# A two-layer graph attention kernel: layer 0's output product of the first and the last step by ordinary products, row tile by row tile, and weight blocks and their sums placed anew

## The chip, the cores and the metric

The kernel runs on one core of a Trainium2 chip. The core has TensorE (PE, with its weight loads shown apart as PEld), VectorE (DVE), ScalarE (ACT), GpSimd (POOL) and SyncE (SP), which here only issues transfers. The metric is the device time of one execution in microseconds (us). One execution was also recorded by the profiler; times inside it are counted from its first instruction.

## The reference, cut to what matters

64 graphs of 256 nodes with 512 features go through two attention layers with a residual. Layer 0 has 4 heads and layer 1 has 8, of 64 each.

```python
h = relu(layernorm(x))
q, k, v = h @ Wq, h @ Wk, h @ Wv                  # layer 0: 512 -> 256
attn = softmax(where(adj, q @ k.T / 8, -max))     # per graph and head
x = x + (attn @ v) @ Wo + bo                      # "combination": 256 -> 512
h = relu(layernorm(x))                            # layer 1 norms once more, with gamma and beta,
x = x + attention1(h, adj | eye) @ w_out.T + b_out #   and has 512 -> 1536 and 512 -> 512
```

The combination of layer 0 is the product that the change touches: for two graphs at a time, 512 rows of 256 numbers by a 256 x 512 matrix, added to the residual.

## The kernel before, in words

**Tiles and steps.** The graphs are taken two by two, in 32 steps (`s` = 0 to 31). Activations of a step stand in tiles of 128 rows; a step has 512 rows, so four row tiles `t`, two for each graph. Everything is float32 but the masks. Each large product (`project_qk`, `project_v1`, `combine`) cuts both factors into 2 x 2 blocks and computes seven block products instead of eight, with sums of blocks prepared beforehand: `weight_sum` for weights, `act_sums0` and `act_sums1` for activations (lines 406 to 414). `PRODUCT` names the two blocks of each of the seven products, and the results are added up while they are copied out of PSUM (`evacuate`, `accumulate`). Only `project_v0` is done by ordinary products, row tile by row tile.

**The order is written by hand.** Every piece of work is put in a list by `at(period, place, fn, ...)`, and the list, sorted by place, is issued in that order on each engine. A period is one step of the steady state and is 6.2 places long; in it the layer-1 work of step p and the layer-0 work of steps p+1 and p+2 alternate on TensorE. `at_dense` puts the products at one place and the copying out (`rest`) shortly after. An engine takes its instructions strictly in this order, so an instruction that waits holds up all that stand behind it. The steady state runs from about the second step to the last but one; the places of the first steps (periods -2 to 0) and of the last (30 and 31) are given one by one.

**PSUM.** Four banks, `m0` to `m3`, take the results of products and transposes in turn (`mm_tile`). A product waits until the former contents of its bank have been copied out. Products 2, 4 and 3 accumulate in the bank of 1, 7 and 5, and wait until those have been copied out.

**The first end.** The weights of layer 1 come from DRAM in four parts (`weight_loads`; q, k, v and the output matrix, parts 0 to 3) and are transposed on TensorE, four blocks for each part: `weight_block(n, c)`, line 468, four transposes into one bank, and two copies out at line 473. Then `weight_sum` makes the three derived blocks and the changed one (line 406). In the kernel before, blocks of parts 0 to 2 stand between the products of steps 0 and 1, and those of part 3 inside the first `project_qk` of layer 1. The sums of `wqkv1[..., 0]` (q), `[..., 1]` (k) and `[..., 2]` (v) and of layer 0's output matrix `wo0` are on VectorE, those of `wo1` on GpSimd.

**Around the combination.** `weigh_out` leaves the attention output in `oT0`; `key_sums`, `invert` and `normalise` divide it by the softmax sums. `invert` (line 945) copies the reciprocals out to 128 partitions in eight transfers on SyncE (line 960), and `normalise` (line 965, GpSimd) multiplies. Then `act_sums0` and `act_sums1` make the sums of `oT0`, and `combine` computes the seven products of 128x256 each. `norm1` (lines 575, 632, 633) takes the mean of a finished row tile on VectorE and the centred rectified row on ScalarE; `norm1_rest` takes the second moments (VectorE) and, for two row tiles together, the scales on GpSimd (lines 648, 649, 585 to 587). `scale_row` (line 591, ScalarE) scales, and `transpose_h` (line 660) transposes for layer 1. `second_bias` (line 637, GpSimd) adds the output bias of layer 1 to the residual.

**The last end.** The last step has no successor to overlap with. Its combination of layer 1 is the end of the program: seven products, and four stores of a quarter of the result each (`store_block`, line 837, on SyncE).

Of the kernel before, what the change touches and what calls it, by code (L numbers as in the profile page):

```python
# [315 lines left out]
def fast_path(  # L316
# [19 lines left out]
    nc = tc.nc  # L336
# [128 lines left out]
    def weight_block(wr, n, c):  # L465
# [3 lines left out]
        for i in range(2):  # L469
            blk = A_OF[i, c // HC]  # L470
            dst = wqkv1[:, blk, c % HC, n, :] if n < 3 else wo1[:, blk, c % HC, :]
            copy = nc.vector.tensor_copy if i == 0 and c % 2 == 0 else nc.scalar.copy
            copy(dst, pw[:, i * H1:(i + 1) * H1])  # L473
# [52 lines left out]
    def neighbours_rows(s):  # L526
        rows = S[s]["rows"] = sm.tile([P, NT, P], BF, name="rows", tag="u", bufs=1)
        for t in range(NT):
            nc.vector.tensor_scalar(rows[:, t, :], onesb, S[s]["any"][:, t:t + 1], None, op0=ALU.mult)
# [182 lines left out]
    def accumulate(n, bank, region, u, last):  # L712
# [11 lines left out]
        elif n == 4:  # L724
            add(r21, bank, r21, ALU.add)  # L725
# [3 lines left out]
        sums = SUM_U_LAST if last else SUM_U  # L729
        if n in sums:  # L730
            r = region[sums[n]]
            (nc.vector if last else nc.gpsimd).tensor_tensor(r, r, u, ALU.add)  # L732

    SUM_U = {7: 3, 3: 1, 4: 2}
    SUM_U_LAST = {6: 1, 7: 3, 4: 2}
# [80 lines left out]
    def combine(s, lyr, n):  # L816
# [14 lines left out]
        at_once = s == NSTEP - 1 or (s, lyr) == (0, 0)  # L831
        return lambda: accumulate(n, bank, token_rows(st["xt"], HD), st["u"], at_once)

    def store_block(s, i, j):

        rows, cols = slice(j * NIC, (j + 1) * NIC), slice(i * HD, (i + 1) * HD)
        nc.sync.dma_start(
            out[s * G + j, :, cols].rearrange("(t p) d -> p t d", p=P), S[s]["xt"][:, rows, cols]
        )
# [197 lines left out]
    for s in range(NSTEP):  # L1037
# [6 lines left out]
        for t in range(NT):  # L1044
            at(p, 0.5 + 0.4 * t if s != 1 else 1.95 + 0.15 * t, norm0, s, t)
# [6 lines left out]
        if s < 2:  # L1052
            at(p, (AT_Q0 + 0.15, 2.72)[s], neighbours_rows, s)
# [6 lines left out]
        at(p, (AT_Q0 + 0.31, 3.75)[s] if s < 2 else 5.7, mask1, s)  # L1060
# [9 lines left out]
        for t in range(NT):  # L1070
            at_dense(p, AT_V0 + 0.14 * t + (-0.0005 if s == 0 and t == 0 else 0 if s != 1 else -0.26 if t < 2 else 0.29), 0.14, project_v0, s, t)
# [5 lines left out]
        at(p, 1.75 if s else 1.8, lambda s=s: act_sums0(S[s]["oT0"]))  # L1077
        at(p, 1.76 if s else 2.48, lambda s=s: act_sums1(S[s]["oT0"]))
        edge = 0 if s == 0 else 1 if s == NSTEP - 1 else 2
        for i, n in enumerate(SETC0 if s else SETC):  # L1080
            if edge == 1:
                at_dense(p, 1.99905 + 0.00008 * i, 0.00107, combine, s, 0, n)
            else:
                at_dense(p, AT_C0 + (-0.12 if s == 0 else 0.14) + i / 14, 1 / 14, combine, s, 0, n)
        for k in range(NT):
            at(p, ((3.315, 3.32, 3.39, 3.41), (2.2, 2.25, 2.4, 2.45), (3.79, 3.8, 3.93, 3.94))[edge][k], norm1, s, k)
            at(
                p, ((3.4, 3.42, 3.43, 3.435), (2.3, 2.35, 2.5, 2.55), (4.075, 4.22, 4.23, 4.36))[edge][k],
# [100 lines left out]
```

## Time and profile before

| what | value |
|---|---|
| median of 3 runs | 3387.38 us (3384.94 to 3389.29) |
| the profiled execution: its time | 3387.59 us |
| the profiled execution: its span, first to last instruction | 3385.8 us |
| PE busy | 3354.9 us (99% of the span) |
| DVE / ACT / POOL busy | 1954.2 / 1232.3 / 2214.4 us (58% / 36% / 65%) |
| mean granted TensorE clock | 0.998 |
| layer 0's combinations and layer 1's, 128x256 products (line 825) | 2688 instructions |

A product of float32 matrices shows as two instructions in this trace, so a block product of `combine` in layer 0 (two row tiles) is 4 instructions, and the whole combination of a step 28. Busy times of PE overlap, since a matmul starts before the one ahead has drained; the distance between two starts is what a matmul costs. Lines of the waits name the engine and line that wait, "<-", and what they waited for, then the us in total, the times and the longest. Lines of the timeline give start, length, engine, line, operation, tiles, shape and number of merged instructions, and in brackets the idle time ahead of it and its releaser.

### The profile page before, as it was taken

How to read it: one execution, taken by the hardware profiler on the slowest of the kernel's cores; microseconds unless marked ns; L12 is line 12 of the kernel's file. 1: busy time of each engine (PE TensorE's matmuls, PEld its weight loads, DVE VectorE, ACT ScalarE, POOL GpSimd, SP SyncE). 2: the span in 40 equal slices, each digit the busy share in tenths (PEclk: the TensorE clock that was granted, in tenths of full speed). 3: DMA queues.
4: the chain of work that ended last, by engine and by line, in shares of the span. 5: the costliest groups of instructions: out<-in, count | busy, mean ns of one | idle time of the engine just before them, and what ended most of it. 6: DMA issues, size and time to landing. Idle time of an engine off the chain costs nothing.

```text
span 3385.8 us, 60239 instructions
## 1 busy us (share of the span) xinstructions
PE 3354.9 (99%) x22986; PEld 2695.6 (80%) x22986; DVE 1954.2 (58%) x3476; ACT 1232.3 (36%) x2225; POOL 2214.4 (65%) x2108
## 2 busy tenths in 40 slices
PE   8999999999999999999999999999999999999999
PEld 6788888888888888788888888887888878888877
DVE  6655565555565555655655555556555565555556
ACT  3333333334433333333343333443333433333421
POOL 6666766667656677566676666765667766667642
PEclk9999999999999999999999999999999999999999
DMA  4111112221111111122111211111211112111111
GB/s 129 43 59 52 33 49 57 57 58 42 46 46 58 57 55 32 47 58 59 52 34 48 58 56 58 42 46 46 58 58 54 32 48 57 59 52 35 45 38 45
DMA packets 167975, 173.97 MB, mean 51 GB/s; under 512 B 59640, under 2 KB 112896, under 8 KB 167680
## 3 DMA queue, kind: packets, MB, share of 16 engines
q1 hardware_dynamic: 167280, 169.78, 17.1%
q8 instruction: 184, 3.01, 0.5%
q14 instruction: 111, 0.91, 0.1%
q10 hardware_dynamic: 400, 0.27, 0.0%
HBM read 85.99 MB, written 33.62 MB: 35 GB/s over the span
## 4 chain that ended last, share of the span: by engine, by line
PE 95%; DVE 1%; DMA 0%; SPq 0%; POOL 0%; ACT 0%; issue 0%; POOLq 0%; ACTq 0%
PE mm L768 33%; PE mm L825 17%; PE mm L809 11%; PE sc L859 11%; PE sc L902 10%; PE mm L795 6%; PE mm L660 3%; PE mm L935 2%; PE mm L548 0%; SPq L960 0%; DVE inv L945 0%; DMA xt<-in_x_dram 0%; DMA out_dram<-xt 0%; DVE p L883 0%; DVE bs L575 0%
## 5 line engine op out<-in xcount | busy, mean ns | idle before, releaser
L893 POOL TENSOR_TENSOR pd<-p 128x512 f32<-128x512 f32 x378 | 473.2, 1273 | 535.2 <-ACT p L888 523.2
L768 PE MATMUL mm<-hT,wqkv 128*128 128x256 f32 x3584 | 801.9, 383 | 3.8 <-DVE qk L700 2.3
L768 PEld LDWEIGHTS mm<-hT,wqkv 128*128 128x128 f32 x3584 | 676.2, 191 | 113.6 <-issue 21.6
L888 ACT ACTIVATE p<-p 128x512 f32<-128x512 f32 x768 | 457.4, 631 | 459.8 <-DVE p L883 457.0
L825 PE MATMUL mm<-wo,oT 128*128 128x256 f32 x2688 | 599.4, 381 | 3.1 <-issue 1.5
L825 PEld LDWEIGHTS mm<-wo,oT 128*128 128x128 f32 x2688 | 501.3, 190 | 82.7 <-DVE xt L721 10.7
L945 DVE RECIPROCAL inv<-mm 128x128 f32<-128x128 f32 x384 | 339.7, 926 | 367.7 <-PE mm L935 346.2
L919 ACT COPY oT<-sc 128x512 f32<-128x512 f32 x188 | 110.0, 585 | 1075.9 <-PE sc L902 1069.3
L883 DVE TENSOR_TENSOR p<-sc,n 128x512 f32<-128x512 f32 x768 | 478.8, 682 | 5.0 <-PE sc L859 5.0
L768 PE MATMUL mm<-hT,wqk 128*128 128x256 f32 x1792 | 398.5, 383 | 0.7 <-ACT wqkv L473 0.6
L809 PE MATMUL mm<-wqkv,hT 128*128 128x256 f32 x1792 | 395.5, 382 | 0.0
L965 POOL TENSOR_TENSOR oT<-oT,invb 128x512 f32<-128x512 f32 x188 | 240.0, 1277 | 222.9 <-DMA invb<-inv 220.8
L768 PEld LDWEIGHTS mm<-hT,wqk 128*128 128x128 f32 x1792 | 337.6, 191 | 57.6 <-issue 10.3
L809 PEld LDWEIGHTS mm<-wqkv,hT 128*128 128x128 f32 x1792 | 338.6, 190 | 54.5 <-issue 10.7
L859 PE MATMUL sc<-qk 64*128 64x256 f32 x3040 | 380.3, 390 | 0.0
L902 PE MATMUL sc<-p,v 128*32 128x256 f32 x6144 | 370.7, 382 | 0.0
L859 PEld LDWEIGHTS sc<-qk 64*128 64x128 f32 x3040 | 278.9, 187 | 103.0 <-issue 64.7
L732 POOL TENSOR_TENSOR xt<-xt,u 128x512 f32<-128x512 f32 x183 | 230.7, 1276 | 165.3 <-DVE xt L725 150.6
L902 PEld LDWEIGHTS sc<-p,v 128*32 128x32 f32 x6144 | 180.7, 110 | 160.9 <-issue 61.7
L721 DVE TENSOR_TENSOR xt<-mm,xt 128x512 f32<-128x512 f32 x128 | 88.2, 689 | 328.1 <-PE mm L825 328.0
L591 ACT ACTIVATE h<-h,mr,r 128x512 f32<-128x512 f32 x252 | 196.9, 807 | 127.9 <-POOL mr L587 123.6
L795 PE MATMUL mm<-wv,hT 128*128 128x256 f32 x1024 | 230.4, 383 | 0.1
(131 smaller groups left out, 3672.7 us busy)
## 6 DMA issues: line engine op xcount, KB each, us to landing
invb<-inv SPq DMA_DIRECT2D x1528, 32.0 KB, 1.9
xt<-in_x_dram SPq DMA_DIRECT2D x32, 1024.0 KB, 5.7
h<-in_x_dram SPq DMA_DIRECT2D x31, 1024.0 KB, 5.4
out_dram<-xt SPq DMA_DIRECT2D x31, 1024.0 KB, 4.5
ne<-row SPq DMA_DIRECT2D x30, 256.0 KB, 4.3
ad<-in_adj_dram SPq DMA_DIRECT2D x32, 128.0 KB, 10.9
wr<-in_L_gnn_w_qkv_dram SPq DMA_DIRECT2D x3, 1024.0 KB, 12.7
h<-in_x_dram SPq DMA_DIRECT2D x4, 256.0 KB, 3.5
```

The lines of the kernel that those rows point to most:

```text
L732: (nc.vector if last else nc.gpsimd).tensor_tensor(r, r, u, ALU.add)
L768: nc.tensor.matmul(bank[:, k, :], w[:, wa, c, k, a * P:(a + 1) * P], st["hT"][:, ba, c, :], start=first and (k, c) == (0, 0), stop=(k, c) ...
L795: nc.tensor.matmul(bank, st["hT"][:, b0 + t // NIC * step, c % HC, i:i + P], wv0[:, c, :], start=(c == 0), stop=(c == NC - 1),)
L809: nc.tensor.matmul(bank[:, t, :], st["hT"][:, ba, c, t * P:(t + 1) * P], wqkv1[:, wa, c, 2, :], start=first and (t, c) == (0, 0), stop=(t, ...
L825: nc.tensor.matmul(bank[:, t, :], oT[:, ba, c, t * P:(t + 1) * P], w[:, wa, c, :], start=first and (t, c) == (0, 0), stop=(t, c) == (NIC - ...
L859: nc.tensor.matmul(sc[g][e][:, kc, :], qk[rows, 1, k0:k0 + P], qk[rows, 0, g * N:(g + 1) * N], start=True, stop=True,)
L883: nc.vector.tensor_tensor(p[e][:, g], sc[e], neg[:, :, g, :], ALU.add)
L888: nc.scalar.activation(p[e][:, g], p[e][:, g], AF.Exp, scale=SCALE)
L893: eng.tensor_tensor(pd[:, e], p[e][:, :, 0, :], p[e][:, :, 1, :], ALU.add)
L902: nc.tensor.matmul(po[r0:r0 + 32, g, :], st[f"v{lyr}"][:, g * NIC + kc, pr * P + r0:pr * P + r0 + 32], p[r0 // DH][:, g, kc, :], start=(kc ...
L945: nc.vector.reciprocal(inv[:, i * P:(i + 1) * P], sums[:, i * P:(i + 1) * P])
L965: nc.gpsimd.tensor_tensor(dst, dst, invb, ALU.mult)
```

## The change

Three things are changed.

1. In the first and the last step, layer 0's combination is done by `combine_rows(s, t)`: for one row tile t, two ordinary products (one for each half of the 256 numbers), each of them 512 columns wide over both halves of the output, and one addition to the residual. No sums of `oT0` and of the output matrix are used there; the copied-out row tile is final, and its `norm1` is placed right behind it. The other steps keep the seven products. `weight_sum` changes block 2 of `wo0`, so for the last step this block is loaded anew in period 29.
2. At the first end the work is placed anew: `neighbours_rows` of step 0 on GpSimd, earlier; the sums of `wo0` and of `wqkv1[..., 2]` on GpSimd, the former in period 0; all weight blocks of parts 1 to 3 between the combination and the transposes for layer 1, with the first of their two copies on VectorE; the sums of `wqkv1[..., 1]` behind part 1; `mask1` of step 1 later, `second_bias` of step 0 in period 0.
3. At the last end, layer 1's combination takes its products in the order 1, 5, 2, 6, 7, 3, 4 instead of 1, 5, 2, 3, 6, 7, 4; both sums with `u` are made right after product 6, the addition after product 4 is done in two halves, and the stores of the last quarters go out in halves on SyncE and ScalarE.

```diff
@@ weight_block
-            copy = nc.vector.tensor_copy if i == 0 and c % 2 == 0 else nc.scalar.copy
+            copy = nc.vector.tensor_copy if i == 0 and (n or c == 0) else nc.scalar.copy
@@ neighbours_rows
-            nc.vector.tensor_scalar(rows[:, t, :], onesb, S[s]["any"][:, t:t + 1], None, op0=ALU.mult)
+            eng = nc.gpsimd if s == 0 else nc.vector
+            eng.tensor_scalar(rows[:, t, :], onesb, S[s]["any"][:, t:t + 1], None, op0=ALU.mult)
@@ accumulate
-            add(r21, bank, r21, ALU.add)
+            for t in range(NIC) if last else (slice(0, NIC),):
+                add(r21[:, t], bank[:, t], r21[:, t], ALU.add)
...
-    SUM_U_LAST = {6: 1, 7: 3, 4: 2}
+    SUM_U_LAST = {6: (1, 2), 7: (3,)}
@@ combine
-        at_once = s == NSTEP - 1 or (s, lyr) == (0, 0)
+        at_once = s == NSTEP - 1
@@ store_block
-        nc.sync.dma_start(
-            out[s * G + j, :, cols].rearrange("(t p) d -> p t d", p=P), S[s]["xt"][:, rows, cols]
-        )
+        dst, src = out[s * G + j, :, cols].rearrange("(t p) d -> p t d", p=P), S[s]["xt"][:, rows, cols]
+        if (i, j) != (1, 0):
+            (nc.scalar if (i, j) == (0, 1) else nc.sync).dma_start(dst, src)
+        else:
+            for t, queue in enumerate((nc.sync, nc.scalar)):
+                queue.dma_start(dst[:, t], src[:, t])
+
+    def combine_rows(s, t):
+
+        st = S[s]
+        g, r = t // NIC, t % NIC * P
+        bank = mm_tile([P, 2, HD])
+        for j, (b0, _, step) in enumerate(O_OF):
+            for c in range(HP0):
+                nc.tensor.matmul(
+                    bank, st["oT0"][:, b0 + g * step, c, r:r + P], wo0[:, j:4:2, c, :],
+                    start=(j, c) == (0, 0), stop=(j, c) == (1, HP0 - 1),
+                )
+        xt = st["xt"][:, t, :].rearrange("p (i o) -> p i o", i=2)
+        return lambda: nc.vector.tensor_tensor(xt, bank, xt, ALU.add)
@@ places
-            at(p, 0.5 + 0.4 * t if s != 1 else 1.95 + 0.15 * t, norm0, s, t)
+            at(p, 0.5 + 0.4 * t if s != 1 else 1.95 + 0.1395 * t, norm0, s, t)
-            at(p, (AT_Q0 + 0.15, 2.72)[s], neighbours_rows, s)
+            at(p, (2.9, 2.72)[s], neighbours_rows, s)
-        at(p, (AT_Q0 + 0.31, 3.75)[s] if s < 2 else 5.7, mask1, s)
+        at(p, (AT_Q0 + 0.31, 4.43)[s] if s < 2 else 5.7, mask1, s)
-            at_dense(p, AT_V0 + 0.14 * t + (-0.0005 if s == 0 and t == 0 else 0 if s != 1 else -0.26 if t < 2 else 0.29), 0.14, project_v0, s, t)
+            at_dense(p, AT_V0 + 0.14 * t + (-0.0005 if s == 0 and t == 0 else 0) if s != 1 else (4.31, 5.02, 5.16, 5.31)[t], 0.14, project_v0, s, t)
-        at(p, 1.75 if s else 1.8, lambda s=s: act_sums0(S[s]["oT0"]))
-        at(p, 1.76 if s else 2.48, lambda s=s: act_sums1(S[s]["oT0"]))
+        if 0 < s < NSTEP - 1:
+            at(p, 1.75, lambda s=s: act_sums0(S[s]["oT0"]))
+            at(p, 1.76, lambda s=s: act_sums1(S[s]["oT0"]))
-        for i, n in enumerate(SETC0 if s else SETC):
-            if edge == 1:
-                at_dense(p, 1.99905 + 0.00008 * i, 0.00107, combine, s, 0, n)
+        for i, n in enumerate(SETC0 if 0 < s < NSTEP - 1 else NORM1):
+            if edge == 0:
+                at_dense(p, 2.76 + 0.14 * i, 0.14, combine_rows, s, n)
+            elif edge == 1:
+                at_dense(p, 1.99905 + 0.00014 * i, 0.00113, combine_rows, s, n)
...
-            at_set(p, LAST_QK + 4.1, (1, 5, 2, 3, 6, 7, 4), combine, s, 1)
+            at_set(p, LAST_QK + 4.1, SETC, combine, s, 1)
-                at(p, LAST_QK + 4.1 + (3, 6, 6, 7)[n] / 7, store_block, s, i, j)
+                at(p, LAST_QK + 4.1 + (3, 6, 5, 7)[n] / 7, store_block, s, i, j)
+    at(NSTEP - 3, 4.5, lambda: nc.sync.dma_start(
+        wo0[:, 2], wo[:HP0 * P, HD:].rearrange("(c p) o -> p c o", p=P)
+    ))
-        at(-2, AT_V0, weight_sum, nc.vector, wo0, i)
+        at(0, 0.9, weight_sum, nc.gpsimd, wo0, i)
-        place = 3.3 - 3.93 + (1 + i) / 7 - 0.0005 if i < 4 else 0.2 + 0.07 * i if i < 8 else 1.62 + 0.1 * (i - 8) if i < 12 else 6.2 + 1 / 7 * (i - 12)
+        place = 3.3 - 3.93 + (1 + i) / 7 - 0.0005 if i < 4 else 1.3705 + 0.0001 * i if i < 8 else 1.525 + 0.03 * (i - 8)
-        at(-1, 3.1 + 0.01 * i, weight_sum, nc.vector, wqkv1[:, :, :, 1, :], i)
-        at(0, 0.2 + i / 7, weight_sum, nc.vector, wqkv1[:, :, :, 2, :], i)
+        at(-1, 1.379 + 0.0001 * i, weight_sum, nc.vector, wqkv1[:, :, :, 1, :], i)
+        at(-1, 1.8, weight_sum, nc.gpsimd, wqkv1[:, :, :, 2, :], i)
```

The places of `norm1`, `norm1_rest`, `scale_row` and `second_bias` in the two edge steps change with it: in the first step `norm1` stands behind each `combine_rows`, and `scale_row` between the weight blocks of parts 1 and 2; in the last step `norm1` stands behind each `combine_rows` too, and `norm1_rest` of the first row tile among them.

## The prediction

> **What bounds the kernel now.** The page's first part says TensorE: 99% of the span. A change away from the steady state can gain only what TensorE loses at the two ends, so I read its waits next, in the first 126 us and in the last 190 (us in total, times, longest).
>
> ```profile
> PE mm L468 <- ACT v L799: 2.6, 1, 2.6
> PE mm L660 <- ACT h L591: 2.5, 5, 0.8
> PE mm L768 <- DVE qk L700: 2.3, 1, 2.3
> PE mm L535 <- DVE rows L529: 1.8, 1, 1.8
> PE mm L825 <- issue: 1.5, 1, 1.5
> PE mm L468 <- ACT wo L473: 1.0, 1, 1.0
> ...
> PE mm L768 <- DVE qk L704: 1.3, 1, 1.3
> PE mm L825 <- DVE xt L721: 0.7, 1, 0.7
> PE mm L825 <- POOL oT L412: 0.4, 1, 0.4
> PE mm L660 <- ACT h L591: 0.4, 1, 0.4
> ```
>
> The first list, which is of 12 to 126 us, sums to 14.0 us with five smaller ones that are left out; the second, of 3200 us on, to 2.8. Third, the timeline, for where they lie and what follows; last, the stretches with the granted clock (length, the engines' busy us, clock, DMA share, GB/s).
>
> ```profile
> 19.85 0.71 PE L535 MATMUL mm<-identb,rows 128*128 128x128 bf16 x4 [1.79 <-DVE rows L529]
> ...
> 109.09 6.41 PE L768 MATMUL mm<-hT,wqkv 128*128 128x256 f32 x16 [2.33 <-DVE qk L700]
> ...
> 96.05 5.81 DVE L406 TENSOR_TENSOR wqkv<-wqkv 128x512 f32<-128x512 f32 x4
> ...
> 3377.28 2.00 PE L825 MATMUL mm<-wo,oT 128*128 128x256 f32 x8 [0.67 <-DVE xt L721]
> ...
> 3380.04 0.69 DVE L732 TENSOR_TENSOR xt<-xt,u 128x512 f32<-128x512 f32 x1
> ```
>
> ```profile
> 87.30:90.70 3.40, 3.31 (x14) 2.76 (x16) 1.75 (x6) 2.19 (x9) 2.57 (x8) 0.50 0.00 0
> ...
> 107.70:114.60 6.90, 5.51 (x13) 4.44 (x14) 4.10 (x6) 1.84 (x5) 6.90 (x6) 0.51 0.06 14
> ```
>
> After two of the waits TensorE runs at half clock for 3.4 and 6.8 us. At 109 us sixteen instructions take 6.41 us where 56 take 12.28 elsewhere (0.22 each, so 3.5): 2.8 us more. Around 87 to 91 us it is some 1.6. With these the first end loses about 19 us behind 12 us. The wait at 109 us is VectorE's: the sums of the k weights (5.81 us for four) stand ahead of what frees the bank.
>
> **What the Trainium skill says.** "TensorE: Matmul & The Clock Gate", What's actually happening: the clock halves after an idle window of about 3.4 us and returns after a busy one. The trace agrees on lengths (3.4 and 6.8 us), but 2.6 us of idle were enough here. Same page, Back-to-back issue gap: warm distance N/2.4 + 2.5 ns, linear in columns N; here the 256-column float32 instruction has 216 ns and a 128-column transpose 109, so linear with two cycles for each column. "SBUF — State Buffer", Who interferes with whom: a VectorE operation with two SBUF inputs and a GpSimd operation exclude each other. The trace agrees: four L406 sums of 128x512 take 4.27 us at 63.29, 5.81 at 96.05 beside GpSimd, and one alone 0.68 at 116.5.
>
> **The change part by part.** I follow TensorE from one point to the next; "was" is the trace.
>
> *Combination.* Was 28 instructions at 0.216 = 6.0 us. Now four row tiles of two products, each two instructions of 512 columns: the trace shows no 512-column float32 instruction. Linear in columns it is 1024/2.4 + 2.5 = 429 ns (an estimate from 216 and 109 ns and the section above), so 16 x 0.429 = 6.9 us: +0.8 at each end. Bounds: 0.427, since 216 is almost twice 109 and leaves no fixed share to save, and 0.85 (half rate), so +0.8 to +7.6 us; I take 0.43.
>
> *First rows (was a 1.79 us wait).* Four 128x128 operations on GpSimd, not shown there; between 0.2 (128x4, L586) and 0.57 us (128x1 power, L605) each, so 0.8 to 2.3. GpSimd is free from 9.74 to 12.01 us and its input is there at 9.4: hidden. If not, the sums of hT behind it come later, with 3 us of room before product 6. The turn starts at 18.0 instead of 19.85: -1.85.
>
> *Transposes of step 1 (were 39.10 to 43.07, 1.8 us of waits).* The four sums of `wo0` (1.79 us at 33.40 on VectorE) and the last moments stood ahead of the row scales; these came at 37.95. Now the moments end near 28.7, since h lands near 23.9 (issue 12.37 plus 11.5), and ScalarE scales the rows behind the exponentials, 33.9 to 37.7. The first product behind them starts at 39.2 instead of 43.07: -3.9 in all. All that follows, GpSimd's work included, moves with it.
>
> *Block 2 of q* is copied by ScalarE alone, so the next product no longer waits for VectorE's reciprocals and that copy (0.56 us and a drain): -4.6. Step 1's seven products end at 61.3 (was 65.94) and its first v tile at 63.1.
>
> *Start of the combination (was 71.28).* The sums of oT0 (four of 0.72 us) are gone. What remains is `normalise`: reciprocals done at 53.0 + 1.8; the eight transfers wait until the former `normalise` ends at 55.2, take 5.0 us to issue and 1.8 to land (were 59.06 to 65.2), so it runs 61.4 to 62.7. The mask that stood ahead of it (3.5 us) now is behind. TensorE is not held: start 63.1, end 70.1, two v tiles to 73.6, four weight blocks (0.44 each) to 75.3.
>
> *The norm chain*, VectorE: each row tile has addition 0.65, and two times moments 0.83, so 2.3; four from 65.0 to 74.8. Then come two copies' worth of waiting: the blocks of k are copied out only now, 0.4 each, and the third v tile waits for the first bank until 75.75 (0.45). Row scales on GpSimd take 1.6 (87.03 to 88.56 plus one), ready at 76.4. ScalarE's copies follow VectorE's (it always waited for L473 of VectorE), to 76.7, then scale two rows (0.75 each), v copy, two rows, to 80.1. VectorE meanwhile does the four k sums: 2.7 us at 0.68, 4.3 at 1.07, 6.6 at 1.65; GpSimd is nearly idle there, so I take 4.3, to 81.0. The blocks of part 3 need banks of part 2, whose copies come behind these sums: TensorE waits from 79.3 to about 82 (2.6 us; 1.2 with sums of 2.7).
>
> *From there:* part 3 to 83.8, scores 2.0, transposes of step 0 at 85.7 instead of 92.72, to 87.6; the weighted sum 1.8. GpSimd's four v sums (1.27 each, from 83 to 88) stand ahead of `key_halves`, so `key_sums` waits some 0.8 (was 0.46): 91. Scores 1.9, then seven products of 12.3 without weight blocks (four were 1.8 us) and without the waits of 1.0 and 2.3 us and the half clock: the next weighted sum starts at 105.5 (was 121.05). **-15.5.** With the faster sums it is -17.1; with the half clock after the 2.6 us wait up to 1.7 less.
>
> *Put at nothing:* `second_bias` (4.95 us) on GpSimd in period 0 eats idle time of 2.83 ahead of the sums of hT(2) (160.65) and part of the next 1.73, so `key_halves` there ends 0.35 late, and TensorE needs it 2 us later; without this cover it were up to 5 us. The sums of `wo0` (2.9) and GpSimd's idle 14.1 us at 114.7. `mask1` is needed a step later. Nobody waits on SyncE behind the load of 128 KB in period 29 (0.4 us to issue); its readers come 70 us later.
>
> *Last step.* Combination +0.8, minus the 0.37 wait for the sums and its drain and the seven switches: it ended at 3266.8 and ends at 3266.7. `norm1` now runs among the row tiles (VectorE free at 3268.75, 0.4 ahead of the reciprocals). So product 4 of the next set finds VectorE free (was 1.33 and drain 0.16), the rows are scaled by 3282 (was 0.37 and two drains), and the weighted sum starts at 3285.1 instead of 3287.78: -2.65. Against it: ScalarE's copy L919 stands behind the last rectified row, ends at 3270.3 instead of 3269.4, and the second half of the scores waits for its bank: +0.4. **-2.25**, and nothing up to 3358 waits, so it is kept.
>
> *Last combination.* Product 3 between 7 and 4 covers the wait of 0.67 and its drain; TensorE ends at 3378.2 (was 3379.2). Behind it were two operations of 0.69 to 3380.73; now two halves of 0.41 (the 128x256 copy of L473), to 3379.0 or sooner: 1.7. The last store of 256 KB, 3.1 us from issue to the event at 3383.9, becomes two of 128 KB, which I count 0.4 us shorter. ScalarE issues two stores; nothing is behind them. **-2.0** in all, cautiously.
>
> Sum: 15.5 + 2.25 + 2.0 = 19.75 us, less 0.2 for stalls of this size that I may not see: 3387.6 - 19.5 = 3368.1 against the profiled execution's own time, which is 0.2 above the median of the runs; so 3368.0.
>
> **Rivals.**
> - *A new wait takes the place of the old ones.* VectorE is the queue of the stage from 65 to 88 us: if its sums meet GpSimd (1.65 each, as beside the first hT sums), the wait for a bank grows to 5 us and half clock follows (1.7), with the POOL sums later too: front 10 us, in all 14: about 3373.5. For it: 96.05's 5.81 us. Against: GpSimd has little to do then.
> - *The advance is not kept.* A transfer or GpSimd in period 0 absorbs it: h of step 2 can be loaded only behind the transposes (issue at 95.36, used at 115). Both move alike, and it lands 5.4 us after issue, so I see no room: within 6 us of before, 3382 to 3387.
> - *Slower: the 512-column product isn't linear.* Place: 32 instructions on the path. Price: each 0.1 us beyond 0.43 costs 3.2 us. From 1.05 us an instruction the gain is gone, at 1.25 it is slower by 0.2%; at 1.7 (a fourth of the rate) the time is 3408. Against it: 216 and 109 ns stand in a line. Other mishaps at the last end, where a SyncE chain of 5 us a unit runs, count here with little.
>
> **How the numbers follow.** Chances: my forecast (3364.5 to 3371.5) 0.66; the new wait (3371.5 to 3378) 0.20; not kept (within 6.8 us, 0.2%, which is about what a measurement can tell from no change) 0.05; slower 0.06; still faster than 3364.5 0.03. So faster 0.89, same 0.05, slower 0.06. The range from 3364.5 to 3377 holds somewhat over 8 in 10; its low end is the free sums and a full last end (17.1 + 2.65 + 2.5), its high end the new wait with lost cover.
>
> **What would show it.** Right: no wait of L535; transposes of h(1) 4 us earlier; a first combination from about 63 to 70 us with 0.43 us an instruction; transposes of step 0 at 84 to 87 us and no half clock behind 100; a wait of L468 for VectorE or ScalarE copies near 80 us as the largest left; at the last end 2 us less from step 31's combination to the weighted sum behind its transposes; last PE instruction straight behind product 3. Wrong: a wait over 3 us between 75 and 90 us, half clock for two windows, instructions of L825's successor over 0.6 us, or new waits in period 0.

## The result and the profile after

The changed kernel takes 3368.47 us, median of 6 runs (3367.26 to 3368.63). The kernel before took 3387.48 us on the same chip (3384.94 to 3390.17). The ratio is 0.9943, with a 95% interval of 0.9930 to 0.9955. That is 19.0 us faster. The prediction was 3368.0. The profiled execution took 3368.43 us with a span of 3366.6 us, against 3387.59 and 3385.8 before.

TensorE is still the bound, at 99% of the span. The waits of TensorE from 12 to 126 us (engine and line that wait, what for, us in total, times, longest):

```profile
PE mm L769 <- DVE qk L705: 0.9, 1, 0.9
PE mm L468 <- ACT wqkv L473: 0.8, 2, 0.6
PE mm L852 <- POOL oT L983: 0.4, 1, 0.4
...
```

With three of 0.3 that are left out they sum to 3.0 us, where the list of before summed to 14.0. None of the former large ones is there. From 3180 us to the end there is none at all. Line numbers have moved: L769 stands for the q and k products, L852 the combination by rows, L920 the weighted sum, L826 the seven-product combination.

The timeline shows where the rest lies (start, length, engine, line, operation, count, and in brackets the idle time ahead of it):

```profile
18.09 0.39 PE L536 MATMUL mm<-identb,rows 128*128 128x128 bf16 x4
...
26.32 1.97 PE L769 MATMUL mm<-hT,wqk 128*128 128x256 f32 x8 [0.88 <-DVE qk L705]
...
64.90 6.28 PE L852 MATMUL mm<-wo,oT 128*128 128x512 f32 x14 [0.39 <-POOL oT L983]
...
81.17 1.97 PE L468 MATMUL mm<-ident,wr 128*128 128x128 f32 x16 [0.60 <-ACT wqkv L473]
...
104.28 1.93 PE L920 MATMUL sc<-p,v 128*32 128x256 f32 x32
...
3252.25 2.69 PE L877 MATMUL sc<-qk 64*128 64x256 f32 x16
```

The neighbour rows are transposed without a wait. The combination is one block from 63.5 to 71.0 us, with a wait of 0.39 us in it. The weighted sum of step 1, the mark of the prediction, starts at 104.28 instead of 121.05 us: 16.77 us sooner. Step 30 still has this advance. Its v product starts at 3230.81 instead of 3247.51.

The stretches with the granted clock (length, the five engines' busy us, clock, DMA share, GB/s):

```profile
60.00:90.00 30.00, 28.44 (x177) 20.17 (x176) 23.47 (x47) 15.99 (x35) 17.50 (x23) 1.00 0.18 51
90.00:126.00 36.00, 36.00 (x248) 28.85 (x246) 23.16 (x42) 7.84 (x14) 21.93 (x25) 1.00 0.15 47
```

Both stretches of half clock are gone, and from 90 us to its last product no wait of TensorE shows.

Set against before, point by point on TensorE. The marks in before, and those in the changed kernel that are not shown yet:

```profile
121.05 1.94 PE L902 MATMUL sc<-p,v 128*32 128x256 f32 x32
...
3287.78 1.93 PE L902 MATMUL sc<-p,v 128*32 128x256 f32 x32
```

```profile
3268.90 1.93 PE L920 MATMUL sc<-p,v 128*32 128x256 f32 x32
...
3346.99 12.36 PE L826 MATMUL mm<-wo,oT 128*128 128x256 f32 x56
```

| stretch | before, us | after, us | difference | predicted |
|---|---|---|---|---|
| start to weighted sum of step 1 | 121.05 | 104.28 | -16.77 | -15.5 |
| from there to the weighted sum behind step 31's transposes | 3166.73 | 3164.62 | -2.11 | -2.25 |
| from there to the end of the last product | 91.50 | 90.45 | -1.05 | -1.0 |
| from there to the end of the span | 6.53 | 7.30 | +0.77 | -1.0 |

The first three rows came out within 1.3 us of the prediction. The last has the other sign. The end of the program was the part to explain.

### The profile page after: what moved, and what is told of

Same layout as the page of the kernel before. It is cut to its first block, busy times and chain, and to the rows that moved or that the text cites. A ratio compares the mean times of both kernels' runs of the same rounds, so it can differ in the third digit from the quotient of the medians.

```text
span 3366.6 us, 60168 instructions
## 1 busy us (share of the span) xinstructions
PE 3349.3 (99%) x22962; PEld 2688.2 (80%) x22962; DVE 1938.0 (58%) x3460; ACT 1230.5 (37%) x2218; POOL 2215.4 (66%) x2112
## 4 chain that ended last, share of the span: by engine, by line
PE 98%; DMA 1%; SPq 0%; DVE 0%; ACT 0%; POOL 0%; issue 0%; POOLq 0%; DVEq 0%
PE mm L769 34%; PE mm L826 17%; PE mm L810 12%; PE sc L877 11%; PE sc L920 11%; PE mm L796 7%; PE mm L661 3%; PE mm L953 2%; PE mm L549 0%; DMA h<-in_x_dram 0%; PE mm L852 0%; SPq L978 0%; DMA wv<-in_L_gnn_Wv_dram 0%; DMA invb<-inv 0%; DVE bs L576 0%; POOL xt L498 0%
## 5 line engine op out<-in xcount | busy, mean ns | idle before, releaser
L769 PE MATMUL mm<-hT,wqkv 128*128 128x256 f32 x3584 | 798.0, 382 | 0.0
L769 PEld LDWEIGHTS mm<-hT,wqkv 128*128 128x128 f32 x3584 | 674.4, 190 | 108.5 <-issue 21.2
L826 PE MATMUL mm<-wo,oT 128*128 128x256 f32 x2632 | 585.7, 381 | 0.0
L826 PEld LDWEIGHTS mm<-wo,oT 128*128 128x128 f32 x2632 | 491.0, 190 | 76.9 <-DVE xt L722 9.7
L769 PE MATMUL mm<-hT,wqk 128*128 128x256 f32 x1792 | 398.9, 383 | 0.9 <-DVE qk L705 0.9
L769 PEld LDWEIGHTS mm<-hT,wqk 128*128 128x128 f32 x1792 | 337.6, 191 | 57.9 <-issue 11.5
L920 PE MATMUL sc<-p,v 128*32 128x256 f32 x6144 | 370.7, 382 | 0.0
L920 PEld LDWEIGHTS sc<-p,v 128*32 128x32 f32 x6144 | 180.7, 110 | 161.3 <-issue 62.0
```

Of the source, the lines that this page charges most:

```text
L769: nc.tensor.matmul(bank[:, k, :], w[:, wa, c, k, a * P:(a + 1) * P], st["hT"][:, ba, c, :], start=first and (k, c) == (0, 0), stop=(k, c) ...
L826: nc.tensor.matmul(bank[:, t, :], oT[:, ba, c, t * P:(t + 1) * P], w[:, wa, c, :], start=first and (t, c) == (0, 0), stop=(t, c) == (NIC - ...
L920: nc.tensor.matmul(po[r0:r0 + 32, g, :], st[f"v{lyr}"][:, g * NIC + kc, pr * P + r0:pr * P + r0 + 32], p[r0 // DH][:, g, kc, :], start=(kc ...
```

## The experiments

The experiments are in three groups: the parts alone with the guard early; the four on the first end; the guard inside, the two waits and the last two. Each group has its own runs of the kernel before on the same chip: 3388.12, 3389.21 and 3387.41 us. Within a group, single executions of the former kernel spread by 3 to 5 us, and those of the kernels with the new first end by 1 to 3. Smaller differences are read inside the traces, between two marks on TensorE.

### The three parts alone

**First end only.** The changed kernel with the last step and the last combination as before:

```diff
-        for i, n in enumerate(SETC0 if 0 < s < NSTEP - 1 else NORM1):
+        for i, n in enumerate(SETC0 if 0 < s else NORM1):
-            at_set(p, LAST_QK + 4.1, SETC, combine, s, 1)
+            at_set(p, LAST_QK + 4.1, (1, 5, 2, 3, 6, 7, 4), combine, s, 1)
...
```

> The changed kernel with its last step and its last combination as they were before the change: only the work of the first end is changed. My theory puts the gain of the first end at 16.7 us, read from the weighted sum of step 1, which starts at 104.28 instead of 121.05 us, and from step 30, which keeps that advance (16.70 us); so 3370.7 us, 16.7 below before. The prediction on record put this part at 15.5 (3372). The rival, that some of the advance is swallowed or that the parts need each other, gives 14 us or less, and then the last end must give 5 us or more.

Measured: 3370.20 us, ratio 0.9946 (0.9932 to 0.9959), so 17.9 us below before. The weighted sum of step 1 starts at 104.15 us. My 16.7 holds, and the rival of 14 or less doesn't. The 1.2 us by which the times give more were not traced; executions of the former kernel with a half clock near 21 us, told of at the end, would account for them.

**Last step only.** The kernel before with `combine_rows` and its norm in step 31:

```diff
-        for i, n in enumerate(SETC0 if s else SETC):
+        for i, n in enumerate(NORM1 if s == NSTEP - 1 else SETC0 if s else SETC):
-                at_dense(p, 1.99905 + 0.00008 * i, 0.00107, combine, s, 0, n)
+                at_dense(p, 1.99905 + 0.00014 * i, 0.00113, combine_rows, s, n)
...
```

> The kernel before with only the last step's combination of layer 0 by ordinary products, its norm placed behind each row tile and the weight block loaded anew. My theory from the two traces is 2.2 us below before (3385.2), with the combination itself 0.8 us longer in its products and shorter in its waits, and the weighted sum behind it 2.2 us nearer to step 30. The rival, that the tail behind TensorE swallows it (the end is set by something that does not move with TensorE), gives 0 to 1 us.

Measured: 3385.55 us, 2.6 below before, ratio 0.9992 (0.9983 to 1.0000), so the times alone barely tell it from no change. In the trace, from the first weighted sum of step 30 to the one behind step 31's transposes it is 58.83 us; before it was 61.00 and in the changed kernel 58.82. So this part alone gives 2.17 us, and it is kept to the end: from there to the last product's end is 91.50 us in this kernel and before.

**Last combination only.** The kernel before with the order of products, sums, half additions and half stores of the change:

```diff
-            at_set(p, LAST_QK + 4.1, (1, 5, 2, 3, 6, 7, 4), combine, s, 1)
+            at_set(p, LAST_QK + 4.1, SETC, combine, s, 1)
-                at(p, LAST_QK + 4.1 + (3, 6, 6, 7)[n] / 7, store_block, s, i, j)
+                at(p, LAST_QK + 4.1 + (3, 6, 5, 7)[n] / 7, store_block, s, i, j)
...
```

> The kernel before with only the last combination of layer 1 changed: its order of products, both sums with u after product 6, the last addition in halves, the last stores in halves on two queues. The prediction on record put this at 2.0 us of gain (3385.4). My theory now is that what ends the program is the check of the largest values with its branch over the general path, which stands behind the last additions once these are the last work: then TensorE ends about 1.0 us earlier but the end comes only 0.3 us earlier (3387.1), which can't be told from no change, and the largest-value reduction, its row transpose and two operations stand behind the last addition, where before they stood ahead of it.

Measured: 3387.54 us, 0.6 below before, ratio 0.9997 (0.9988 to 1.0005): not told from no change. In the trace the last stretch of TensorE is 90.45 us, 1.05 less than before, and what follows takes 6.84 us instead of 6.53. TensorE's gain is there and is partly given back.

### What ends the program

Behind the last addition stands the guard: the largest absolute values are reduced, transposed as one row (L1179) and compared (L1181, L1182). Each engine loads the flag (L1183) and branches (L1184) over the general path that would be run for large values. In the kernel before, the row's transpose lay ahead of the last product and the comparison ended at 3378.1 us, before the last addition. So it is in all four traces with the former order of products; in the seven with the new order and this guard, all of it falls behind the last product. VectorE in the changed kernel at the end:

```profile
3359.39 0.76 DVE L727 TENSOR_TENSOR xt<-mm,xt 128x256 f32<-128x256 f32 x2 [1.03 <-PE mm L826]
3360.06 0.27 DVE L1181 TENSOR_REDUCE all_top<-row 1x1 f32<-1x128 f32 x1
3360.36 0.14 DVE L1182 TENSOR_SCALAR safe<-all_top 1x1 int32<-1x1 f32 x1
```

The instructions of the branch's line (engine, operation, ns shortest/median/longest, first and last start in us):

```profile
L1184 DVEq COMPARE_BRANCH  x1: 72/72/72, 3361.2 to 3361.2; - x1
...
L1184 DVEq EVENT_SEMAPHORE  x1: 21/21/21, 3365.6 to 3365.6; - x1
```

VectorE branches 1.0 us after its last addition and goes on 4.5 us later. ScalarE takes 4.2 us for its jump, GpSimd and SyncE 0.5. The last store was issued at 3360.2. From the last addition's end to the span's end it is 6.5 us; before it was 5.1 (3380.73 to 3385.8).

SyncE shows which of these ends the program. At the end of the program it first waits for the transfers, then collects a signal of each engine. Both steps in before, then in the changed kernel:

```profile
L1158 SPq EVENT_SEMAPHORE  x8: 17/17/17, 3383.9 to 3384.4; - x8
...
L1184 SPq EVENT_SEMAPHORE  x10: 17/28/28, 3384.5 to 3385.8; - x10
```

```profile
L1184 SPq EVENT_SEMAPHORE  x8: 17/17/17, 3361.6 to 3362.3; - x8
...
L1210 SPq EVENT_SEMAPHORE  x10: 17/28/2982, 3362.4 to 3366.6; - x10
```

In before the last store, issued at 3380.8, held it until 3383.9, and then every signal was there. In the changed kernel the stores are done by 3362.3, and it waits 2.98 us for VectorE's signal behind the jump, at 3365.6. So the end passed from the store to the guard and the jump.

**The guard early.** All of it ahead of the last combination:

```diff
+    def guard():
+        nc.vector.tensor_reduce(top, extremes, axis=mybir.AxisListType.X, op=ALU.max)
+        row = mm_tile([1, P])
+        nc.tensor.transpose(row, top, ident)
+        nc.vector.tensor_reduce(all_top, row, axis=mybir.AxisListType.X, op=ALU.max)
+        nc.vector.tensor_scalar(safe, all_top, LIMIT, None, op0=ALU.is_le)
+    at(NSTEP - 2, LAST_QK + 4.04, guard)
...
```

> The changed kernel with the check of the largest values (its reduction, the row transpose on TensorE, and two operations on VectorE) issued ahead of the last combination instead of behind the last additions; nothing is left out, the flag is still loaded and branched on at the end. If the check sets the end, as I think, the flag is ready 10 us before the last product ends, and the program ends 0.5 to 1.5 us sooner than the changed kernel (3367.0 to 3368.0), the transpose costing 0.3 us in the middle of that gain. If the last stores set the end, it is the same or 0.1 to 0.3 us slower (3368.5 to 3368.8).

Measured: 3369.71 us, ratio 0.9945 (0.9932 to 0.9959). No gain. The waits from 3180 us on show why:

```profile
PE mm L1152 <- DVE top L1150: 3.1, 1, 3.1
```

The reduction stands on VectorE behind the sums of `oT1`, which end at 3349.1 us, and TensorE waited for it ahead of the combination. That was the fault of this placing. The end itself did get shorter: from the last product's end to the span's end it is 6.22 us instead of 7.30.

**The guard inside.** The reduction at the same place, the rest between the third and the fourth product:

```diff
+    at(NSTEP - 2, LAST_QK + 4.04, lambda: nc.vector.tensor_reduce(scalars[0], extremes, axis=mybir.AxisListType.X, op=ALU.max))
+    at(NSTEP - 2, LAST_QK + 4.1 + 2.95 / 7, guard)
...
```

> The changed kernel with the check of the largest values inside the last combination: the reduction on VectorE ahead of it, the row transpose on TensorE between its third and fourth product, the two operations on VectorE behind it. The earlier placing made TensorE wait 3.1 us for that reduction and so could not show what the end is worth; here the reduction is done 3 us before the transpose. My theory: no wait on TensorE, 0.1 to 0.3 us for the transpose in the middle, and the stretch from the end of the last product to the end of the span 6.2 us as there instead of 7.25: 0.7 to 1.0 us sooner than the changed kernel. The rival: the jump of VectorE and ScalarE over the general path, which starts behind the last addition and the last store in any case, sets the end, and the stretch stays above 6.8 us.

Measured: 3367.14 us; the changed kernel on the same chip 3367.54. TensorE doesn't wait, and the last end is 6.45 us. The difference of the times, 0.4, is below what they can tell, so I go by this stretch in all traces. With the new last combination and the guard behind it, it is 6.5 to 7.3 us (seven traces, mean 6.90). With the former one it is 6.06 to 6.53 (four, mean 6.34), and with the guard moved 6.13 to 6.45 (three, mean 6.27). So the guard's place is worth 0.6 us, the size that the new last combination had lost. The rival (above 6.8) falls, though not all of its idea: the jump of VectorE starts behind its last addition and takes 3.0 to 4.0 us with the guard moved too, and this can't be hidden by moving the guard. In the three kernels with the guard moved ScalarE's signal is the last, 0.4 to 1.2 us behind VectorE's: it branches only when it has issued its half of the last store.

### What at the first end gives the gain

**Seven products at the new places.** The changed kernel, step 0 with `combine`:

```diff
+        if s == 0:
+            at(p, 2.4499, lambda s=s: act_sums0(S[s]["oT0"]))
+            at(p, 2.45, lambda s=s: act_sums1(S[s]["oT0"]))
...
-                at_dense(p, 2.76 + 0.14 * i, 0.14, combine_rows, s, n)
+                at_dense(p, 2.76 + 0.08 * i, 0.08, combine, s, 0, n)
...
-        at(0, 0.9, weight_sum, nc.gpsimd, wo0, i)
+        at(-2, 6.015, weight_sum, nc.gpsimd, wo0, i)
...
```

> The changed kernel, but the first step's combination is done by the seven products again, at the new places (behind the third v tile's predecessor, with the weight blocks behind it); the sums of oT0 stand right behind the normalisation, those of the output matrix of layer 0 on GpSimd early. My theory is that the row-by-row form is what makes the new places work: a row tile is final after one addition, so the moments and the row scales of the norm start at once, while the seven products finish all four row tiles only at the end and give VectorE some 4 us more to do. Then this kernel is 5 to 7 us slower than the changed one (about 3374 to 3376). The rival, that the placing alone gives the gain and the ordinary products cost their 0.8 us, makes it 0.8 us faster than the changed one (about 3368).

Measured: 3373.80 us, ratio 0.9959 (0.9945 to 0.9972). The weighted sum of step 1 starts at 110.63 us, 6.35 later than in the changed kernel. Its two largest waits, and VectorE's busy time (the third of the five) in the stretch that ends with the first of them:

```profile
PE mm L826 <- DVE xt L722: 2.7, 1, 2.7
PE mm L468 <- ACT v L800: 2.2, 1, 2.2
```

```profile
68.00:72.40 4.40, 1.72 (x8) 1.17 (x7) 4.30 (x5) 0.00 (x0) 4.23 (x5) 1.00 0.00 0
```

VectorE is busy in 4.30 of 4.40 us of the first stretch. With the seven products the sums with `u` and the additions come first: the first moments start at 74.0 and the last end at 81.2 us, 5.1 us later than in the changed kernel. Behind the second wait a half clock comes back, from 81.5 to 84.9 us (shown at the end). The expectation of 5 to 7 us holds, and the rival, that placing is the whole gain, falls.

**Rows at the old places.** The kernel before with `combine_rows` in step 0:

```diff
+            elif edge == 0:
+                at_dense(p, AT_C0 - 0.12 + 0.125 * i, 0.125, combine_rows, s, n)
-        at(-2, AT_V0, weight_sum, nc.vector, wo0, i)
+        at(0, 0.9, weight_sum, nc.gpsimd, wo0, i)
...
```

> The kernel before with only the first step's combination row tile by row tile: the norm behind each tile, no sums of oT0, the output matrix's sums on GpSimd in period 0; weight blocks, k and v weight sums, masks and neighbour rows stay where they were. My theory: it gains only 4 to 6 us of the first end's 16.7 (about 3382 to 3384), since the waits for the k weight sums and for the blocks of part 3 at 90 to 121 us and the half clock behind them stay. The rival, that the form of the combination is the gain, gives 10 us or more (3378 or less).

Measured: 3382.97 us, 6.2 below before, ratio 0.9983 (0.9977 to 0.9990). The weighted sum of step 1 starts at 117.05, 4.0 us sooner than in the profile of before. Two waits that the changed kernel doesn't have are left as they were:

```profile
PE mm L768 <- DVE qk L700: 2.3, 1, 2.3
...
PE mm L468 <- ACT wo L473: 1.0, 1, 1.0
```

The profile of this kernel has a half clock near 21 us that the profile of before lacks (told of at the end). Two other profiles with the old front do have it, those of the last step and of the last combination alone. Against their 123.24 and 122.56 us this kernel is 6.2 and 5.5 sooner, in line with the 6.2 of the times. So I take some 6 us for the form alone, a little more than the 4 to 6 that I expected. At the new places it gives 6.35 (110.63 to 104.28), and placing alone gives 10.4 (121.05 to 110.63). Within what the half clocks leave open, the two add up, and neither needs the other. My theory ahead of these runs said more, that the form is what makes the new places work; this is not so. The rival of 10 us or more for the form alone falls as well.

**Neighbour rows back on VectorE.**

```diff
-            eng = nc.gpsimd if s == 0 else nc.vector
+            eng = nc.vector
-            at(p, (2.9, 2.72)[s], neighbours_rows, s)
+            at(p, (AT_Q0 + 0.15, 2.72)[s], neighbours_rows, s)
```

> The changed kernel with the neighbour rows of step 0 on VectorE at their former place. The wait of 1.79 us ahead of the transposes at 19.85 us should come back, so the turn starts 1.8 us later; if nothing behind it swallows this, the time is 1.8 us above the changed kernel (3370.3). If the late landing of h of step 1 caps what an earlier start is worth, as the wait of 0.88 us at 26.3 us suggests, it is 0.9 us above (3369.4), and that wait is gone.

Measured: 3369.01 us, ratio 0.9944 (0.9930 to 0.9957), not told apart from the changed kernel by time. In the trace the wait is back:

```profile
19.87 0.71 PE L536 MATMUL mm<-identb,rows 128*128 128x128 bf16 x4 [1.79 <-DVE rows L530]
```

The wait of 0.88 us at 26.3 is gone, and the weighted sum of step 1 starts at 105.03: 0.75 us later, not 1.85. The late landing of h, with VectorE's moments of h ahead of the addition L705, caps what the earlier start is worth.

**GpSimd's sums beside VectorE's.**

```diff
-        at(0, 0.9, weight_sum, nc.gpsimd, wo0, i)
+        at(-1, 1.3785, weight_sum, nc.gpsimd, wo0, i)
```

> The changed kernel with GpSimd doing the four sums of layer 0's output matrix at the same time as VectorE does the four sums of the k weights, instead of 35 us later. This puts the rival of my prediction on the chip: the k sums then take 5 us or more in place of 2.95 us for four, the wait for a bank near 81 us grows from 0.6 to 2 or 3 us, with or without half clock behind it (up to 1.7 us more), and the weighted sum of step 1 comes 2 to 4 us later, the whole 2 to 4 us above the changed kernel (3370.5 to 3372.5). The other answer, that the two engines don't hinder each other here or that the stage has room, leaves the k sums under 3.5 us and the time the same.

Measured: 3368.92 us, ratio 0.9943 (0.9929 to 0.9956). The k sums and the block behind them:

```profile
76.35 4.26 DVE L406 TENSOR_TENSOR wqkv<-wqkv 128x512 f32<-128x512 f32 x4
...
81.40 1.97 PE L468 MATMUL mm<-ident,wr 128*128 128x128 f32 x16 [1.76 <-ACT wqkv L473]
```

In the changed kernel the sums take 2.95 us and this wait is 0.60. With GpSimd at work they take 1.3 us more, and TensorE waits 1.2 us more. There is no half clock behind it. So the hindrance is real, but smaller than I expected. As the combination didn't have to wait in this execution, the weighted sum came only 0.24 us later than in the changed kernel (104.52).

### Two waits that were left

```diff
-            at(p, 0.5 + 0.4 * t if s != 1 else 1.95 + 0.1395 * t, norm0, s, t)
+            at(p, 0.5 + 0.4 * t if s != 1 else (2.0835, 2.09, 2.229, 2.3685)[t], norm0, s, t)
-            at(p, ((2.901, 3.041, 3.181, 3.321), (1.99919, 1.99933, 1.99947, 1.99961), (3.79, 3.8, 3.93, 3.94))[edge][k], norm1, s, k)
+            at(p, ((2.901, 3.041, 3.181, 3.321), (1.99919, 1.99933, 1.99947, 2.1), (3.79, 3.8, 3.93, 3.94))[edge][k], norm1, s, k)
```

> The changed kernel with two waits taken away by order alone. The moments of h of step 1 stand behind the addition that frees the bank, so the wait of 0.88 us at 26.3 us should go, and the weighted sum of step 1 come 0.9 us sooner (103.4 instead of 104.28). The rectified row of the last row tile of step 31 stands behind the copy that frees the bank of the scores, so the scores at 3252 us take 2.0 instead of 2.69 us and the next products start 0.69 us sooner behind step 30's. Together 1.6 us (3366.9). The rival for each: the work put behind is late in its turn and its reader waits as long; then the marks stand where they stood.

Measured: 3364.92 us, ratio 0.9936 (0.9922 to 0.9949), and the changed kernel on the same chip 3367.54: 2.6 us sooner. VectorE in the changed kernel (its second profile, on this chip), and then in this one:

```profile
24.43 0.69 DVE L576 BATCH_NORM_STATS2 bs<-h 128x6 f32<-128x512 f32 x1 [2.08 <-DMA h<-in_x_dram]
...
25.26 0.66 DVE L705 TENSOR_TENSOR qk<-mm,qk 128x512 f32<-128x512 f32 x1
```

```profile
23.31 0.69 DVE L705 TENSOR_TENSOR qk<-mm,qk 128x512 f32<-128x512 f32 x1 [1.03 <-PE mm L769]
24.45 0.69 DVE L576 BATCH_NORM_STATS2 bs<-h 128x6 f32<-128x512 f32 x1 [0.45 <-DMA h<-in_x_dram]
```

VectorE waited 2.08 us for h with the addition L705 behind it in the queue, and TensorE waited 0.99 us for the bank that L705 frees. Now L705 comes first. The transposes of step 1 start 1.30 us sooner (35.95 against 37.25); a wait of 0.23 at 48 us goes too, and the first v tile starts 1.59 sooner. Here the combination found the normalisation done, where it had waited 0.54 us, so the weighted sum comes 2.26 us sooner. That last step is not shown to belong to the edit: the transfers of the reciprocals landed in 2.4 instead of 2.95 us behind the end of their issue, and the wait was 0 to 0.54 us in the kernels that kept this stage. The kernel with all together, below, has neither this wait nor that for L705.

At the last step the scores take 2.00 us again, and from the combination to the next products it is 11.18 us instead of 11.88: 0.70, as expected.

**All together**, both orders and the guard inside:

```diff
+            at(p, 0.5 + 0.4 * t if s != 1 else (2.0835, 2.09, 2.229, 2.3685)[t], norm0, s, t)
...
+    at(NSTEP - 2, LAST_QK + 4.1 + 2.95 / 7, guard)
...
```

> The changed kernel with both waits taken away and the check of the largest values inside the last combination. If the three add up, 2.3 to 2.6 us sooner than the changed kernel: 3366.0, or 21.5 below before. If the guard's place is worth nothing, 1.6 us (3366.9).

Measured: 3364.61 us (3364.41 to 3365.74), ratio 0.9934 (0.9921 to 0.9948): 2.9 us below the changed kernel and 22.8 below before. Both marks moved as in the kernel with two waits (the weighted sum of step 1 is at 102.32 us), and the last end is 6.13 us. The branch of VectorE, and where ScalarE goes on, in the same view as above:

```profile
L1190 DVEq COMPARE_BRANCH  x1: 72/72/72, 3357.6 to 3357.6; - x1
...
L1190 ACTq EVENT_SEMAPHORE  x1: 17/17/17, 3361.9 to 3361.9; - x1
```

VectorE branches right behind the last addition, which ends at 3357.5, and goes on at 3360.8; ScalarE comes 1.1 us later. Set against the kernel with two waits alone (3364.92), the guard's share is not resolved by the times. These two are the fastest versions here.

**The changed kernel once more**, without an edit, for the comparison:

> The changed kernel itself on the same chip, so that the three others, which differ from it by 1 to 3 us, can be set against it: 19.0 us below before, as in its first runs.

Measured: 3367.54 us, ratio 0.9941 (0.9928 to 0.9955): 19.9 below before.

## Why the prediction was right, and which step was wrong

The forecast of 19.55 us against 19.2 between the two spans is right partly because two errors have opposite signs. The first end gave 1.3 us more and the last combination 1.7 less than put down, and the 0.2 set aside for unseen stalls brought the sum nearer. So it is in part luck that the number is this close.

**512-column products: right.** In step 31 they start 0.435 us apart (16 from 3243.00 to 3249.96 us); the estimate was 0.429. The rival in which this form is not linear falls. (The 1.6 and 2.8 us of half clock and the waits of 14.0 us sum to 18.4, which I called about 19.)

**First rows: the mechanism right, the sum wrong as a separate term.** GpSimd took 2.35 us for its four, a little above the bound of 2.3, and was hidden. But the turn's 1.85 us can't be added to what follows: with the rows put back, 0.75 is lost. The first product behind the transposes of step 1 came 3.65 us sooner, not 3.9.

**h of step 1: a wait that I hadn't seen.** I let h land near 23.9 us; VectorE's first moments start at 24.69, and in the traces with this front between 24.0 and 26.0. The moments stood ahead of L705, and TensorE waited 0.88 us (0.4 to 1.5 in five other kernels with this order, none in a sixth). So this is the largest wait left, and not the one of L468 near 80 us that I named, which is 0.60.

**Combination: the start 0.4 us late, and it was held.** The v tile ahead of it came 4.2 us sooner, not 4.6. I wrote that TensorE is not held. From the first issue of the reciprocals' transfers to `normalise` it took 7.75 us (55.84 to 63.59), where I had taken over the 6.2 us to the landing in before. So it ran at 63.59 instead of 61.4, and TensorE waited 0.39.

**k sums and the wait for a bank: mis-sized.** I took 4.3 us though I had written that GpSimd is nearly idle there. They took 2.95, and the wait was 0.60 instead of 2.6. With GpSimd made busy they do take 4.26, and the wait is 1.76. So 4.3 was the price for a case that I had myself excluded: the sums of 4.27 us at 63.29 us, from which it comes, had GpSimd's masks beside them. The bound of 2.7 was the right choice (its wait of 1.2 would give -16.9, not -17.1). The wait of `key_sums` was 0.26 instead of 0.8. Together these are 2.5 us, and since TensorE came to the blocks of part 3 1.3 us later than put down (80.6 instead of 79.3), 1.3 us are left.

**The new wait as a rival: its mechanism exists, its price was too high.** No half clock followed its 1.76 us.

**Put at nothing: right.** No wait appears in period 0, and step 30 has the advance but for 0.07 us. Half clock is gone.

**Last step: right.** -2.17 alone and -2.11 in the sum against -2.25. The 0.4 for the copy behind the last rectified row was 0.69.

**Last combination: the step that failed.** TensorE ended 1.05 us sooner, and the additions end 0.79 us behind it instead of 1.45. So 1.7 us sooner in all, as predicted. Then I let the store set the end and counted 0.4 us for it. The stores are indeed done sooner, but the end is now VectorE's jump behind the guard. What follows the last addition grew from 5.1 to 6.5 us; over all traces the means are 4.9 us with the former order, 6.1 with the new one and 5.5 with the guard moved. So the guard's place explains half of the growth. For the other half no run takes the cause away; there ScalarE's signal is the last. I had written of its two stores that nothing is behind them, but its load of the flag and its jump are. The part gave 0.3 us in the profile, and 0.6, not told from none, when done alone. The row transpose at 3376.34 us on TensorE stood ahead of the last product in the profile of before. It moved with the order of products, and I hadn't counted it among the moved instructions. Why it does so is not shown: the kernel's text has it behind all products in both.

**Open:** why the jump of VectorE and ScalarE over the general path takes 2.5 to 4.5 us and varies. The Trainium skill ("Runtime: NRT & Kernel Launch", Instruction fetch mechanics) says that a taken branch to a place that isn't loaded must first fetch it by DMA, and gives no time. The trace fits in part: between the branches at 3361.2 us and VectorE's going on at 3365.6 the queues of the kind "instruction" move 5 packets, 0.05 MB, but they are done by 3363.6. No kernel here took the jump away. VectorE's took 3.6 to 4.5 us in the seven kernels where all engines branched at once, and 2.9 to 3.3 in six of the others. The seventh has 4.0, so this is not shown to be the reason.

## What to carry to other kernels

Look for what the last work had been covering: when the last product moves up, whatever stood in the gap ahead of it (here a guard) becomes the end. A wait for a transfer is cheap only if nothing behind it in that engine's queue frees a bank; put the additions that free banks first. A cheaper form of a product can be worth less than a form whose results are final early: the ordinary products take 6.96 us on TensorE in step 31, against 6.35 for the seven of a step in the steady state, and gave some 6 us at the first end.

## What the runs showed of the hardware

**Half clock follows from TensorE's idle time within one stretch of a fixed grid, not from the length of one wait.** In each of the 14 traces the changes of the granted clock lie whole multiples of 3.41 us apart. Where the clock was full and TensorE was idle for 1.98 us or more of one such stretch (21 cases, the program's end among them), the next stretch had half clock. With 1.89 us or less it never had. At half clock less was enough: three stretches with 1.15 to 1.35 us of idle time were followed by another.

So a longer wait can cost less. The kernel with the guard early waits 3.10 us, from 3346.5 to 3349.6. Its clock changes at 17.01 and 3365.49 us, 981 stretches apart, so a border lies at 3348.42: 1.89 us of the wait are on one side, 1.21 on the other, and the clock stays full. The wait of 2.21 us in the kernel with seven products at the new places lies within one stretch but for 0.2 us, and with smaller gaps this stretch is idle for 2.33 us. The stretches of the two (length, TensorE's busy us first, clock third from the end):

```profile
3345.01:3348.42 3.41, 1.52 (x31) 0.65 (x20) 2.34 (x4) 0.00 (x0) 0.00 (x0) 1.00 0.00 0
3348.42:3351.84 3.42, 2.21 (x11) 2.01 (x12) 1.49 (x5) 0.13 (x1) 0.00 (x0) 1.00 0.00 0
...
78.09:81.51 3.42, 1.09 (x8) 0.86 (x8) 3.28 (x10) 1.55 (x5) 1.46 (x5) 1.00 0.00 0
81.51:84.92 3.41, 2.98 (x7) 2.44 (x8) 3.24 (x7) 2.78 (x6) 2.10 (x5) 0.50 0.00 0
```

The grid lies elsewhere in each execution. In the profile of before the wait for the neighbour rows is 1.79 us, too short for it, and the clock stays full. In three kernels with the same front this wait was 2.3 to 2.5 us, 2.2 to 2.5 of it within one stretch. Half clock followed, and 40 products took 10.56 us instead of 8.87. So the former kernel can lose 1.7 us more than its profile shows; no profile of its own shows it. The changed kernel doesn't have this wait. The Trainium skill ("TensorE: Matmul & The Clock Gate", What's actually happening) puts the halving down to an idle window of about 3.4 us. The lengths agree, but here 2 us of idle time in such a window were enough.

**A jump over code that isn't run takes 2.5 to 4.5 us on VectorE and ScalarE**, and 0.2 to 0.5 us on GpSimd, in all traces here.
